# Wider moving blocks for ScalarE's quarter of a layer's product, and a norm's Newton steps on GpSimd

## The chip, the cores and the metric

The kernel runs on one core of a Trainium2 chip. The metric is the device time of one execution in microseconds, from its start to the end of its last output; several executions are timed, and their median counts. A profile of one execution gives the span (first to last instruction), what each engine did when, and what each wait was for. The engines are TensorE (PE in the profile, its weight loads PEld), VectorE (DVE), ScalarE (ACT), GpSimd (POOL) and SyncE (SP), which issues most of the DMAs.

## What is computed

Two graph layers on x of 8 batches, 2048 nodes and 64 features, with one sparse 2048 x 2048 adjacency matrix whose rows are normalized. Layer 0 has weights and a bias of its own for each node, mixed from 16 shared ones by an embedding; layer 1 has one weight for all. Each layer adds its input and is normalized over the features. Cut to what matters:

```python
def _layernorm(x, axis=-1, eps=1e-5):
    m = jnp.mean(x, axis=axis, keepdims=True)
    v = jnp.var(x, axis=axis, keepdims=True)
    return (x - m) / jnp.sqrt(v + eps)

def _L0_gnn_ref(x, A, embedding, weight, bias):      # K = 3, D = 16
    w = jnp.einsum('nd,dkio->nkio', embedding, weight)
    b = jnp.einsum('nd,do->no', embedding, bias)
    # A_stack: identity, A, 2 A A - identity
    x_g = jnp.einsum('knm,bmc->bnkc', A_stack, x)
    return jnp.einsum('bnki,nkio->bno', x_g, w) + b

x = _layernorm(x + _L0_gnn_ref(x, adj, embedding0, weight0, bias0))
x = _layernorm(x + _L1_gnn_ref(x, adj, adj, weight1, bias1))
```

## The kernel before

The program runs in stages: two hops over the adjacency matrix for layer 0, layer 0's product with its weights (lines 394 to 441, called from the loop at 834), and two hops for layer 1. The change is in the product. It goes over 16 tiles of 128 nodes (`t` from 0 to 15).

For a tile, `mix0` multiplies the three inputs (x, first hop, second hop) by the 16 shared weights, and sums over the 16 with each node's embedding as factor. Inputs and weights are split into three parts each (high, low, mixed; `parts` at line 308, `w_parts`), so that an input times a weight is three matmuls. The eight batches lie as four pairs: two batches of a pair are on the lower and the upper 64 partitions, and a matmul uses 64 rows of the array. Matmuls therefore come in pairs `j` = 0, 1, on the two halves of the array, into two neighbouring banks of PSUM.

The work of a tile is cut into eight pieces `(g, dg)`: `g` is a half of the batches (two pairs, `i` = 0, 1) and `dg` a group of DG = 4 of the 16 weights. A piece fills one buffer of two PSUM banks, of which there are four in rotation (`bank`, shared with the transposes `pt` and the projection `pu`). It takes 36 matmuls with 256 moving columns (4 weights of 64 columns): 2 `i` x 3 inputs x 3 parts x 2 `j`. Then it is evicted: with `dg` = 0 by ScalarE (line 429), four operations of 128x256 that scale by the embedding and write to a buffer `aside`; else by VectorE (line 431), four multiply-and-add operations of 128x256 into the accumulator `acc`. In tile 15 ScalarE takes `dg` = 0 and 1. GpSimd folds an `aside` in two steps (line 403: 512, then 256 elements) and adds it to `acc` (line 400).

The order on each engine is as written: in this part of the program `ordered` keeps the recorded order of all instructions but the matmuls, whose order is also that of the source. Each engine takes its instructions strictly in turn, so an instruction that waits holds up all behind it on its engine. The dictionary `at` says which other work is recorded before which piece: the preparation of the next tile's parts (`of_x`, `of_hop`, `of_second`), the steps `n1`, `n2`, `n3` of the previous tile's norm, the start of the next tile's sum (`begin_sum`, GpSimd), the multiplication by the matrix's values (`times_r`, GpSimd), the transposes of the previous tile's normalized rows (`hT`), and in tile 15 the operands of the next stage (`early`, on ScalarE and VectorE, with DMAs from SP). After the pieces the previous tile is projected with layer 1's weights (`project`), and ScalarE copies the result out.

The norm (`layernorm`, line 359) sums a row on VectorE, subtracts the mean on GpSimd, squares on ScalarE, sums the squares on VectorE, takes the root on ScalarE, and then takes 1/root on VectorE and refines it by one Newton step (`rsqrt_parts`, lines 325 to 346; four small VectorE operations of 128x8 besides the reciprocal). GpSimd multiplies by it (line 374).

```python
ds = slice(dg * DG, (dg + 1) * DG)
pm = bank("pm").rearrange("p j (i d c) -> p j i d c", i=2, d=DG)
...
if dg < on_act:
    ordered(nc.scalar.activation(to[:, d], got, AF.Copy, scale=e))
else:
    ordered(nc.vector.scalar_tensor_tensor(part, got, e, part, ALU.mult, ALU.add))
```

Of the kernel before, what the change touches and what calls it, by code (L numbers as in the profile page):

```python
# [9 lines left out]
F32 = mybir.dt.float32  # L10
# [3 lines left out]
AF = mybir.ActivationFunctionType  # L14
ALU = mybir.AluOpType
# [3 lines left out]
P = 128  # L19
B, N, C = 8, 2048, 64  # L20
NT = N // P
D = 16
DG = 4
EPS = 1e-5
# [15 lines left out]
def pattern(  # L40
# [22 lines left out]
    nc = tc.nc  # L63
# [5 lines left out]
    work = pool(ctx, "fwork", 2)  # L69
# [14 lines left out]
    def bank(name):  # L84

        return psum.tile([P, 2, 512], F32, tag="ps", name=name)
# [40 lines left out]
    def ordered(ins):  # L127
        if in_order:
            tc.keep_in_program_order(ins)
# [173 lines left out]
    def transpose(src, tag, pt=None):  # L303

        tt = xcpool.tile([P, B // 2, P], F32, tag="ln_xc", name=tag)
        ordered(nc.scalar.copy(by_half(tt), transposed(src, pt)))
        return tt
# [15 lines left out]
    def wide(c):  # L323
        return c.unsqueeze(2).to_broadcast([P, B, C])

    def rsqrt_parts(ss):


        def col(name):
            m = max(B, ss.shape[1])  # L330
            return (work if m == B else keep).tile(list(ss.shape), F32, tag=f"{name}{m}", name=name)

        va = col("ln_v")
        ordered(nc.vector.scalar_tensor_tensor(va, ss, 1.0 / C, eps.to_broadcast(list(ss.shape)), ALU.mult, ALU.add))
        sd = col("ln_sd")
        ordered(nc.scalar.activation(sd, ss, AF.Sqrt, bias=eps, scale=1.0 / C))
        yield None
        r0 = col("ln_r0")
        ordered(nc.vector.reciprocal(r0, sd))

        q = col("ln_q")
        ordered(nc.vector.scalar_tensor_tensor(q, r0, -0.5, r0, ALU.mult, ALU.mult))
        ordered(nc.vector.tensor_tensor(q, q, va, ALU.mult))
        r = col("ln_r")
        ordered(nc.vector.scalar_tensor_tensor(r, q, 1.5, r0, ALU.add, ALU.mult))
        yield r
# [12 lines left out]
    def layernorm(src):  # L359

        s = work.tile([P, B], F32, tag="ln_s", name="s")
        ordered(nc.vector.tensor_reduce(s, src, AX.X, ALU.add))
        ordered(nc.vector.tensor_tensor(s, s, part, ALU.mult))
        xc = xcpool.tile([P, B, C], F32, tag="ln_xc", name="xc")
        ordered(nc.gpsimd.tensor_tensor(xc, src, wide(s), ALU.subtract))  # L365
        yield xc.rearrange("p b c -> p (b c)")
        sq = squares(xc)
        yield
        ss = work.tile([P, B], F32, tag="ln_ss", name="ss")
        ordered(nc.vector.tensor_reduce(ss, sq, AX.X, ALU.add))  # L370
        root = rsqrt_parts(ss)
        next(root)
        yield
        ordered(nc.gpsimd.tensor_tensor(xc, xc, wide(next(root)), ALU.mult))
        yield

    def store(t, r):
# [13 lines left out]
            ))  # L391
        return acc

    def mix0(t, tt, acc, at, on_act=1):

        aside = [None, None]

        def add_aside(g):
            part = acc[:, 4 * g : 4 * g + 4, :]
            ordered(nc.gpsimd.tensor_tensor(part, part, aside[g][:, 0], ALU.add))  # L400

        def summed(one, other, n):
            ordered(nc.gpsimd.tensor_tensor(one[:, :n], one[:, :n], other, ALU.add))  # L403

        for g in range(2):
            part = acc[:, 4 * g : 4 * g + 4, :]
            for dg in range(D // DG):
                if (g, dg) == (1, 2 if on_act == 1 else 0):
                    add_aside(0)
                for work_here in at.get((g, dg), ()):  # L410
                    work_here()
                ds = slice(dg * DG, (dg + 1) * DG)
                pm = bank("pm").rearrange("p j (i d c) -> p j i d c", i=2, d=DG)
                for i in range(2):
                    for k in range(3):
                        for n in range(3):
                            for j in range(2):
                                q = slice(j * C, (j + 1) * C)
                                nc.tensor.matmul(  # L419
                                    pm[:, j, i], lhsT=tt[k][n][q, 2 * g + i, :], rhs=w_parts[n][k][q, ds, :],  # L420
                                    start=(k == 0 and n == 0), stop=(k == 2 and n == 2),
                                )
                if dg < on_act:
                    to = rawp.tile([P, DG, B // 2, C], F32, tag="raw", name="aside")
                for d in range(DG):
                    dd = dg * DG + d
                    got, e = pm[:, :, :, d, :].rearrange("p j i c -> p (j i) c"), emb_sb[:, t, dd : dd + 1]
                    if dg < on_act:
                        ordered(nc.scalar.activation(to[:, d], got, AF.Copy, scale=e))  # L429
                    else:  # L430
                        ordered(nc.vector.scalar_tensor_tensor(part, got, e, part, ALU.mult, ALU.add))  # L431
                if dg < on_act:
                    if dg == 0:
                        aside[g] = to
                    else:
                        summed(aside[g], to, DG)
                    if dg == on_act - 1:
                        for n in (2, 1):
                            summed(aside[g], aside[g][:, n : 2 * n], n)
        add_aside(1)  # L440
        return layernorm(acc)

    def project(t, hT, pus=None):
# [245 lines left out]
    def times_r(t):  # L689
        to = z2[:, t, :].rearrange("p (j n) -> p j n", n=P)  # L690
        r = rrow[:, t * P : (t + 1) * P].unsqueeze(1).to_broadcast([P, B // 2, P])
        ordered(nc.gpsimd.tensor_tensor(to, to, r, ALU.mult))  # L692
# [9 lines left out]
    def operands(t, quick=False):  # L702

        xt = work2.tile([P, B // 2, P], F32, tag="t0", name="xt")
        load(nc.sync, xt, xT[t])
        tt = [None] * 3

        def begin(k, src):
            where, tag = ((rawp, "raw"), (spool, "s"))[k != 2]
            high = hpool.tile([P, B // 2, P], F32R, tag="hl", name="hl")  # L710
            pair = where.tile([P, 2, B // 2, P], F32R, tag=tag, name="parts")
            tt[k] = [high, pair[:, 0], pair[:, 1]]
            return parts(src, tt[k], by_half if k == 1 else lambda to: to, quick)

        def of_x():
            yield from begin(0, xt)

        def of_hop(pt=None):
            yield from begin(1, transposed(z[1][t], pt))

        def of_second():
            yield from begin(2, by_pair(z[2][t]))

        return tt, of_x(), of_hop, of_second()
# [102 lines left out]
    def go(it):  # L827
        return lambda: next(it)
# [4 lines left out]
    coming = operands(1)  # L833
    for t in range(NT):
        got, last = {}, t == NT - 1
        at = {(g, dg): [] for g in range(2) for dg in range(D // DG)}
        n1, n2, n3 = [lambda: next(norm)] * 3 if t else [nothing] * 3

        if not last:
            following, of_x, of_hop, of_second = coming  # L840
            of_hop = of_hop()
            at[0, 1] += [go(of_x)] * (1 if t else 3)
            at[0, 2] += [go(of_hop), n1, go(of_hop), go(of_hop), n2]
            if t + 2 < NT:
                at[0, 2] += [lambda: times_r(t + 2)]
                at[1, 0] += [lambda: got.update(coming=operands(t + 2))]
            at[0, 3] += [n3, go(of_second), lambda: got.update(acc=begin_sum(t + 1))]
            at[1, 0] += [go(of_second), go(of_second)]
            at[1, 3] += [lambda: got.update(hT=transpose(h, "hT"))] if t else []
        else:  # L850
            at[0, 1] += [n1, lambda: early(0, *y, *s)]
            at[0, 2] += [n2, lambda: early(1, *y, *s)]
            at[0, 3] += [n3, lambda: early(2, *y)]
            at[1, 0] += [lambda: early(3, *y)]
            at[1, 1] += [lambda: early(4, *y)]
            at[1, 2] += [lambda: got.update(hT=transpose(h, "hT"))]
            at[1, 3] += [lambda: project(t - 1, got["hT"])]
        norm_now = mix0(t, tt, acc, at, 2 if last else 1)
        if 0 < t < NT - 1:
            project(t - 1, got["hT"])  # L860
        if "coming" in got:
            coming = got["coming"]
            next(coming[1])
            next(coming[1])
        norm = norm_now
        h = next(norm)
        if not last:
            tt, acc = following, got["acc"]
# [480 lines left out]
```

## Time and profile before

| what | us |
|---|---|
| median of three executions | 769.81 (767.96 to 770.3) |
| the profiled execution | 768.76 |
| its span | 767.0 |
| layer 0's product in it | 226.8 to 533.7 |
| one tile of it, from tile to tile | 19.15 |
| TensorE granted clock | 0.997 of full speed |

Busy times of the engines in one stretch of 19 us inside the product (321 to 340 us): TensorE 19.00, VectorE 16.67, ScalarE 9.43, GpSimd 13.98; DMA engines 6%. The last stretch, 511.0 to 533.6, has TensorE busy 21.0 of 22.6 us.

How to read the lines: a line of a chain gives start, length, engine, tile and source line; a line of a group gives the source line, the engine and operation, output and inputs with their shape (partitions x elements), the count, the busy time and mean duration in ns, and after the second bar the idle time of the engine ahead of them and what ended it. In the timeline a row with "x36" runs from the first instruction's start to the last one's end, and matmuls overlap, so that a row's length is not a sum. Instructions that only wait, or that issue a DMA, are not counted as busy.

### The profile page before, as it was taken

The numbers are of one execution on the slowest core, as the hardware profiler recorded it, in microseconds if no ns is written. First come the engines' busy times: TensorE is split into PE (matmuls) and PEld (weight loads), VectorE is DVE, ScalarE is ACT, GpSimd is POOL, SyncE is SP. The second block draws the span as 40 slices with busy tenths as digits, with TensorE's granted clock in tenths as the row PEclk, the third lists the DMA queues.
The fourth block names the chain that finished last, engine by engine and source line by source line (L and its number), as shares of the span: only waits on it lengthen the run. The fifth ranks groups of instructions, "written<-read, shape, count | busy, mean of one in ns | idle before, by whom it ended". The sixth has DMA issues, their size and how long they took to land.

```text
span 767.0 us, 18011 instructions
## 1 busy us (share of the span) xinstructions
PE 757.0 (99%) x7246; PEld 674.8 (88%) x7246; DVE 582.8 (76%) x1222; ACT 387.7 (51%) x760; POOL 252.5 (33%) x247
## 2 busy tenths in 40 slices
PE   8999999999999999999999999999999999999996
PEld 6888888888889999999999999998888888888886
DVE  6778766677758898888889888876688648668664
ACT  4446533878744555555545555547787763112111
POOL 0000000000026777777777777766100000012341
PEclk9999999999999999999999999999999999999998
DMA  8998996555510000000000000002354444565731
GB/s 308 374 389 294 340 313 209 164 168 164 171 60 27 20 8 19 20 17 16 17 16 10 20 17 3 3 29 70 127 168 146 138 149 137 178 183 164 217 128 45
DMA packets 73546, 96.77 MB, mean 126 GB/s; under 512 B 4848, under 2 KB 48368, under 8 KB 73328
## 3 DMA queue, kind: packets, MB, share of 16 engines
q1 hardware_dynamic: 62048, 76.66, 30.7%
q10 hardware_dynamic: 11408, 18.89, 6.6%
q8 instruction: 59, 0.97, 0.5%
q14 instruction: 31, 0.25, 0.1%
HBM read 76.65 MB, written 18.87 MB: 125 GB/s over the span
## 4 chain that ended last, share of the span: by engine, by line
PE 96%; DVE 2%; DMA 1%; ACT 1%; POOL 0%; issue 0%; SPq 0%; POOLq 0%; DVEq 0%
PE pm L419 35%; PE accT L641 27%; PE acc L254 15%; PE a L254 10%; PE accT L254 6%; PE pu L451 2%; DMA raw<-in_adj 1%; PE pt L300 1%; DVE acc L431 1%; PE accT L791 1%; DVE hl L238 0%; PE accT L451 0%; ACT aside L429 0%; SPq L123 0%; POOL xc L365 0%
## 5 line engine op out<-in xcount | busy, mean ns | idle before, releaser
L419 PE MATMUL pm<-wh,hl 64*128 64x256 f32 x1536 | 235.4, 286 | 0.7 <-DVE acc L431 0.7
L419 PE MATMUL pm<-wm,parts 64*128 64x256 f32 x1536 | 230.9, 280 | 0.0
L419 PE MATMUL pm<-wl,parts 64*128 64x256 f32 x1536 | 230.8, 280 | 0.0
L641 PE MATMUL accT<-s,hl 128*128 128x512 f32 x896 | 205.7, 390 | 0.0
L431 DVE SCALAR_TENSOR_TENSOR acc<-pm,pack_sb,acc 128x256 f32<-128x256 f32 x376 | 181.5, 483 | 27.5 <-PE pm L419 14.1
L641 PEld LDWEIGHTS accT<-s,hl 128*128 128x128 f32 x896 | 167.6, 188 | 35.4 <-issue 0.2
L419 PEld LDWEIGHTS pm<-wh,hl 64*128 64x128 f32 x1536 | 160.3, 188 | 1.2 <-PE pt L300 0.8
L419 PEld LDWEIGHTS pm<-wl,parts 64*128 64x128 f32 x1536 | 160.2, 188 | 0.0
L419 PEld LDWEIGHTS pm<-wm,parts 64*128 64x128 f32 x1536 | 160.0, 187 | 0.0
L629 ACT CAST s<-raw 128x1024 fp32r<-128x1024 bf16 x104 | 109.7, 1055 | 38.0 <-ACT hl L234 24.7
L254 PE MATMUL acc<-hl,s 128*128 128x512 f32 x512 | 117.3, 390 | 0.6 <-DVE s L223 0.6
L254 PEld LDWEIGHTS acc<-hl,s 128*128 128x128 f32 x512 | 95.8, 188 | 21.8 <-issue 1.0
L692 POOL TENSOR_TENSOR z<-z,rrow 128x512 f32<-128x512 f32 x16 | 21.1, 1319 | 213.0 <-DVE z L665 213.0
L429 ACT ACTIVATE aside<-pm,pack_sb 128x256 f32<-128x256 f32 x136 | 53.3, 475 | 54.0 <-PE pm L419 54.0
L234 ACT CAST hl<-z 128x256 fp32r<-128x256 f32 (+1 forms) x96 | 47.4, 511 | 63.4 <-PE acc L254 24.7
L403 POOL TENSOR_TENSOR aside<-aside 128x512 f32<-128x512 f32 (+2 forms) x66 | 70.5, 1068 | 18.4 <-ACT aside L429 15.7
L254 PE MATMUL a<-hl,s 128*128 128x512 f32 (+1 forms) x352 | 73.4, 370 | 0.0
L254 PEld LDWEIGHTS a<-hl,s 128*128 128x128 f32 x352 | 61.9, 188 | 11.3
L238 DVE TENSOR_TENSOR hl<-z,hl 128x512 fp32r<-128x512 f32 (+1 forms) x96 | 54.6, 576 | 14.0 <-ACT hl L234 11.4
L320 POOL TENSOR_TENSOR parts<-parts 128x512 fp32r<-128x512 f32 x45 | 57.7, 1294 | 11.6 <-DVE parts L314 9.8
L287 POOL TENSOR_TENSOR z<-z,got 128x512 f32<-128x512 f32 x3 | 4.8, 1622 | 143.8 <-ACT got L286 143.8
L254 PE MATMUL accT<-hl,s 128*128 128x512 f32 x192 | 44.3, 390 | 0.0
(129 smaller groups left out, 822.9 us busy)
## 6 DMA issues: line engine op xcount, KB each, us to landing
raw<-in_adj SPq DMA_DIRECT2D x59, 512.0 KB, 5.6
raw<-sums_of SPq DMA_DIRECT2D x64, 256.0 KB, 2.7
sums_of<-z ACTq DMA_DIRECT2D x16, 512.0 KB, 6.1
raw<-quarters SPq DMA_DIRECT2D x32, 256.0 KB, 2.7
raw<-in_adj SPq DMA_DIRECT2D x16, 384.0 KB, 3.0
quarters<-seen ACTq DMA_DIRECT2D x16, 256.0 KB, 5.7
xt<-in_xT SPq DMA_DIRECT2D x16, 256.0 KB, 2.6
z<-in_x SPq DMA_DIRECT2D x15, 256.0 KB, 6.9
```

Source lines behind the costliest of these rows:

```text
L234: ordered(nc.scalar.copy(to[0], src))
L238: ordered(nc.vector.tensor_tensor(to[1], src, to[0], ALU.subtract))
L254: nc.tensor.matmul(accs[i], lhsT=s[:, i * P : (i + 1) * P], rhs=hl[h], start=(first and h == 0), stop=(last and h == 1),)
L320: ordered(nc.gpsimd.tensor_tensor(mixed, mixed, low, ALU.add))
L403: ordered(nc.gpsimd.tensor_tensor(one[:, :n], one[:, :n], other, ALU.add))
L419: nc.tensor.matmul(pm[:, j, i], lhsT=tt[k][n][q, 2 * g + i, :], rhs=w_parts[n][k][q, ds, :], start=(k == 0 and n == 0), stop=(k == 2 and n ...
L429: ordered(nc.scalar.activation(to[:, d], got, AF.Copy, scale=e))
L431: ordered(nc.vector.scalar_tensor_tensor(part, got, e, part, ALU.mult, ALU.add))
L451: nc.tensor.matmul(pm[:, j, i * 3 * C : (i + 1) * 3 * C], lhsT=hT[q, 2 * g + i, :], rhs=v[q], start=True, stop=True,)
L629: ordered(nc.scalar.copy(s, got["raw"]))
L641: nc.tensor.matmul(acc[i][:, c], lhsT=hl[h][:, i * P : (i + 1) * P], rhs=S[:, c * 512 : (c + 1) * 512], start=(kk == 0 and h == 0), stop=( ...
L692: ordered(nc.gpsimd.tensor_tensor(to, to, r, ALU.mult))
```

## The change

`mix0` gets a list of pieces instead of two loops. ScalarE's share of a half `g` is now cut by batch, not by weights: piece `(g, 0)` or `(g, 1)` multiplies one pair of batches by eight weights, 512 moving columns, in 18 matmuls, and ScalarE evicts it by eight operations of 128 elements into two `aside` buffers that both pieces of a half share. VectorE's pieces `(g, 2)` to `(g, 5)` are the former `dg` = 0 to 3. In tiles 0 to 14 ScalarE has the two pieces of half 0, at the tile's head and as the fifth piece; all of half 1 goes to VectorE. In tile 15 it has both pieces of both halves. GpSimd folds a half's two buffers in one go (1024, 512, 256 elements and the addition to `acc`), once a tile instead of twice, and ahead of the seventh piece (in tile 15 ahead of the fourth and the eighth).

The norm inside the product no longer calls `rsqrt_parts`: VectorE keeps the reciprocal, and five small operations go to GpSimd. In tile 15 `n3` moves up to the third piece, the transposes to the sixth and the projection to the seventh.

```diff
-        root = rsqrt_parts(ss)
-        next(root)
+        sd, r0, va, q, r = [work.tile([P, B], F32, tag=f"{name}{B}", name=name) for name in ("ln_sd", "ln_r0", "ln_v", "ln_q", "ln_r")]
+        ordered(nc.scalar.activation(sd, ss, AF.Sqrt, bias=eps, scale=1.0 / C))
         yield
-        ordered(nc.gpsimd.tensor_tensor(xc, xc, wide(next(root)), ALU.mult))
+        ordered(nc.vector.reciprocal(r0, sd))
+        ordered(nc.gpsimd.tensor_scalar(va, ss, -0.5 / C, -0.5 * EPS, ALU.mult, ALU.add))
+        ordered(nc.gpsimd.tensor_tensor(q, r0, r0, ALU.mult))
+        ordered(nc.gpsimd.tensor_tensor(q, q, va, ALU.mult))
+        ordered(nc.gpsimd.tensor_scalar(q, q, 1.0, 1.5, ALU.mult, ALU.add))
+        ordered(nc.gpsimd.tensor_tensor(r, q, r0, ALU.mult))
+        ordered(nc.gpsimd.tensor_tensor(xc, xc, wide(r), ALU.mult))
         yield
...
-    def mix0(t, tt, acc, at, on_act=1):
+    def mix0(t, tt, acc, at, pieces):
+        def block(pm, lhsT, ds):
+            for k in range(3):
+                for n in range(3):
+                    for j in range(2):
+                        q = slice(j * C, (j + 1) * C)
+                        nc.tensor.matmul(
+                            pm[:, j], lhsT=tt[k][n][q, lhsT, :], rhs=w_parts[n][k][q, ds, :],
+                            start=(k == 0 and n == 0), stop=(k == 2 and n == 2),
+                        )
...
+        def by_batch(g, i):
+            pm = bank("pm").rearrange("p j (d c) -> p j d c", c=C)
+            block(pm, 2 * g + i, slice(0, 2 * DG))
+            if i == 0:
+                aside[g] = [rawp.tile([P, DG, 2, 2, C], F32, tag="raw", name="aside") for _ in range(2)]
+            for d in range(2 * DG):
+                ordered(nc.scalar.activation(aside[g][d // DG][:, d % DG, :, i, :], pm[:, :, d, :], AF.Copy, scale=e(d)))
+
+        def by_four(g, dg):
+            dg -= 2
+            pm = bank("pm").rearrange("p j (i d c) -> p j i d c", i=2, d=DG)
+            for i in range(2):
+                block(pm[:, :, i], 2 * g + i, slice(dg * DG, (dg + 1) * DG))
+            for d in range(DG):
+                part = acc[:, 4 * g : 4 * g + 4, :]
+                got = pm[:, :, :, d, :].rearrange("p j i c -> p (j i) c")
+                ordered(nc.vector.scalar_tensor_tensor(part, got, e(dg * DG + d), part, ALU.mult, ALU.add))
...
         def add_aside(g):
+            one, other = [a.rearrange("p d j i c -> p d (j i) c") for a in aside[g]]
             part = acc[:, 4 * g : 4 * g + 4, :]
+            for to, more in ((one, other), (one[:, :2], one[:, 2:]), (one[:, 0], one[:, 1]), (part, one[:, 0])):
+                ordered(nc.gpsimd.tensor_tensor(to, to, more, ALU.add))
...
+            at[6] += [0]
+            at[7] += [lambda: got.update(hT=transpose(h, "hT"))] if t else []
+            pieces = [(0, 0), (0, 4), (0, 5), (1, 2), (0, 1), (1, 3), (1, 4), (1, 5)]
         else:
...
+            at[1] += [n1, lambda: early(0, *y, *s)]
+            at[2] += [n2, n3, lambda: early(1, *y, *s)]
+            at[3] += [0, lambda: early(2, *y)]
+            at[4] += [lambda: early(3, *y)]
+            at[5] += [lambda: early(4, *y), lambda: got.update(hT=transpose(h, "hT"))]
+            at[6] += [lambda: project(t - 1, got["hT"])]
+            at[7] += [1]
+            pieces = [(0, 0), (0, 1), (0, 4), (1, 0), (1, 1), (0, 5), (1, 4), (1, 5)]
```

A number in `at` stands for `add_aside` of that half.

More of the change, by code (lines that the diff above doesn't have):

```diff
@@ L392, in begin_sum, with e @@
         return acc
-    def mix0(t, tt, acc, at, on_act=1):
-        aside = [None, None]
+    def mix0(t, tt, acc, at, pieces):
[8 more added lines that the diff above has]
+                        )
+        def e(d):
+            return emb_sb[:, t, d : d + 1]
+        def by_batch(g, i):
[14 more added lines that the diff above has]
+                ordered(nc.vector.scalar_tensor_tensor(part, got, e(dg * DG + d), part, ALU.mult, ALU.add))
+        aside = {}
@@ L398, in add_aside @@
         def add_aside(g):
+            one, other = [a.rearrange("p d j i c -> p d (j i) c") for a in aside[g]]
             part = acc[:, 4 * g : 4 * g + 4, :]
[L400 to L410, printed above, removed]
-                    work_here()
[L412 to L439, printed above, removed]
@@ L440, in mix0 @@
-        add_aside(1)
+            for to, more in ((one, other), (one[:, :2], one[:, 2:]), (one[:, 0], one[:, 1]), (part, one[:, 0])):
+                ordered(nc.gpsimd.tensor_tensor(to, to, more, ALU.add))
+        for n, (g, i) in enumerate(pieces):
+            for work_here in at[n]:
+                if isinstance(work_here, int):
+                    add_aside(work_here)
+                else:
+                    work_here()
+            (by_batch if i < 2 else by_four)(g, i)
         return layernorm(acc)
@@ L835, in pattern @@
         got, last = {}, t == NT - 1
-        at = {(g, dg): [] for g in range(2) for dg in range(D // DG)}
+        at = [[] for _ in range(8)]
         n1, n2, n3 = [lambda: next(norm)] * 3 if t else [nothing] * 3
@@ L841, in pattern @@
             of_hop = of_hop()
-            at[0, 1] += [go(of_x)] * (1 if t else 3)
-            at[0, 2] += [go(of_hop), n1, go(of_hop), go(of_hop), n2]
+            at[1] += [go(of_x)] * (1 if t else 3)
+            at[2] += [go(of_hop), n1, go(of_hop), go(of_hop), n2]
             if t + 2 < NT:
[L845 to L849, printed above, removed]
-        else:
[L851 to L858, printed above, removed]
+                at[2] += [lambda: times_r(t + 2)]
+                at[4] += [lambda: got.update(coming=operands(t + 2))]
+            at[3] += [n3, go(of_second), lambda: got.update(acc=begin_sum(t + 1))]
+            at[4] += [go(of_second), go(of_second)]
+            at[6] += [0]
+            at[7] += [lambda: got.update(hT=transpose(h, "hT"))] if t else []
+            pieces = [(0, 0), (0, 4), (0, 5), (1, 2), (0, 1), (1, 3), (1, 4), (1, 5)]
+        else:
+            at[1] += [n1, lambda: early(0, *y, *s)]
[6 more added lines that the diff above has]
+            pieces = [(0, 0), (0, 1), (0, 4), (1, 0), (1, 1), (0, 5), (1, 4), (1, 5)]
+        norm_now = mix0(t, tt, acc, at, pieces)
         if 0 < t < NT - 1:
```

## The prediction

> **What bounds the kernel now.** I read the page's totals first, then the chain of waits in order of time for the stage that the change touches (226.8 to 533.7 us), then single stretches of the timeline, then the groups kept apart by shape. The totals:
>
> ```profile
> span 767.0 us, 18011 instructions
> PE 757.0 (99%) x7246; PEld 674.8 (88%) x7246; DVE 582.8 (76%) x1222; ACT 387.7 (51%) x760; POOL 252.5 (33%) x247
> ```
>
> TensorE is busy for 99% of the span. That alone doesn't prove a bound, so the chain, here over one tile of layer 0's product and into the next (start, length, what):
>
> ```profile
> 340.48 4.31 PE pm L419 x72
> 345.03 10.85 PE pm L419 x180
> 356.12 2.20 PE pm L419 x36
> 358.32 1.30 PE pu L451 x16
> 359.63 4.31 PE pm L419 x72
> ```
>
> Each link is TensorE's own work, and the same five links repeat every 19.15 us. One tile is 144 pairs of matmuls, 1.30 us of projection and two sets of transposes. So in tiles 0 to 14 only TensorE's own time counts, as long as no buffer comes free late. Its spacing is in the timeline:
>
> ```profile
> 341.25 0.30 PE L419 MATMUL pm<-wm,parts 64*128 64x256 f32 x2
> ...
> 342.45 0.30 PE L419 MATMUL pm<-wh,hl 64*128 64x256 f32 x2
> ...
> 119.63 2.66 PE L254 MATMUL acc<-hl,s 128*128 128x512 f32 x11
> ...
> 579.67 3.11 PE L641 MATMUL accT<-s,hl 128*128 128x512 f32 x13
> ...
> 754.52 6.02 PE L254 MATMUL a<-hl,s 128*128 128x256 f32 x48
> ```
>
> The first two lines are ten pairs apart: 1.20/10 = 120.0 ns a pair of 256 columns. A row of n matmuls lasts (n-1) spacings and one duration (390 ns at 512 columns, 284 at 256, from the groups), so 512 columns take (2.66-0.39)/10 = 227.0 and (3.11-0.39)/12 = 226.7 ns, and 256 columns on the full array (6.02-0.284)/47 = 122.0 ns. Doubling the columns from 122.0 adds 104.7, not 122.0: about 17 ns belong to the matmul, not to its columns.
>
> Two places where TensorE does wait lie in the last tile (waits of this stage: total, times, longest):
>
> ```profile
> PE pt L300 <- POOL xc L374: 0.9, 1, 0.9
> PE pm L419 <- DVE acc L431: 0.7, 1, 0.7
> ```
>
> What prices the other engines' edits is in the groups by shape (busy, mean ns | idle before):
>
> ```profile
> L429 ACT ACTIVATE aside<-pm,pack_sb 128x256 f32<-128x256 f32 x136 | 53.3, 475 | 54.0 <-PE pm L419 54.0
> L403 POOL TENSOR_TENSOR aside<-aside 128x512 f32<-128x512 f32 x32 | 41.6, 1299 | 12.4 <-ACT aside L429 12.2
> L403 POOL TENSOR_TENSOR aside<-aside 128x256 f32<-128x256 f32 x32 | 23.9, 748 | 2.5
> L403 POOL TENSOR_TENSOR aside<-aside 128x1024 f32<-128x1024 f32 x2 | 5.0, 2483 | 3.4 <-ACT aside L429 3.4
> ```
>
> and two lines of the timeline, of which the second shows VectorE held up beside GpSimd:
>
> ```profile
> 370.41 1.04 POOL L374 TENSOR_TENSOR xc<-xc,ln_r 128x512 f32<-128x512 f32 x1 [0.51 <-DVE ln_r L345]
> ...
> 520.50 2.25 DVE L238 TENSOR_TENSOR hl<-z,hl 128x256 fp32r<-128x256 f32 x1 [1.67 <-ACT hl L234]
> ```
>
> **What the Trainium skill says.** "TensorE: Matmul & The Clock Gate", section "Back-to-back issue gap", gives N/2.4 + 2.5 ns for an isolated matmul: 109.2 at 256 columns, 215.8 at 512. The trace agrees that there is a fixed part and has it larger: 120.0 and 226.7. "VectorE: DVE Perf Modes", in its section on the TRN2 errata, prices a ScalarE operation out of PSUM at 172 cycles plus one per element at 1.2 GHz: 357 ns at 256, 250 at 128; the trace has 365 at 256 ((1.57-0.475)/3 in a row of four). "SBUF — State Buffer", section "SBUF: two separate sides", says that GpSimd and a VectorE operation with two SBUF inputs exclude each other for a whole instruction. The trace agrees: the VectorE line above took 2.25 us where its kind takes 0.42, beside a GpSimd addition of 1024 elements.
>
> **The change, part by part.**
>
> *Moving blocks.* In tiles 0 to 14 two of eight pieces become 9 pairs of 512 columns in place of 18 of 256; in tile 15 four do. The trace has no pair of 512 columns on half arrays, so I bound it. Not cheaper per column: 240.0 ns, no gain. At the skill's 215.8: 24.2 gained a pair. I take 226.7, what a 512-column matmul costs here on the full array, because at 256 columns the half-array pair (120.0) and the full-array matmul (122.0) cost nearly the same. Gain: 240.0-226.7 = 13.3 ns a pair, 18 x 13.3 = 239 ns a tile, 15 x 0.239 = 3.6 us. The tile goes from 19.15 to 18.91 us.
>
> *ScalarE's eviction.* 8 operations of 128 elements a piece instead of 4 of 256: 8 x 0.25 + 0.1 = 2.1 us against 1.57, twice a tile, some 1 us more on an engine that is busy 9.6 of 19 us. Piece 0's bank is wanted again by piece 3, 4.6 us after piece 0 ends: 2.5 us are spare. Piece 4's, by piece 7, has about as much.
>
> *GpSimd's sums.* Before: 2 x (1.299 + 0.748 + 0.769) = 5.63 us a tile. After: 2.483 + 1.299 + 0.748 + 0.769 = 5.30 us, all behind piece 4's eviction (done 13.1 us into the tile) and behind the second hop's parts (15.4): they end at 20.7, that is 1.8 us into the next tile. The next norm's sum reads the accumulator, but stands on VectorE behind a subtraction that waits for ScalarE until 1.7 and ends at 2.4 (361.99 before, in a tile begun at 359.63). So 0.5 us are spare; beyond that the delay is still only VectorE's, which waits 1.1 us for TensorE there.
>
> *Newton steps.* VectorE loses four operations (in the timeline 0.27+0.43+0.17+0.17 = 1.0 us). GpSimd gains five on 128x8. No such row exists there: the slope of the additions is (1299-748)/256 = 2.15 ns an element, which leaves some 0.2 us fixed; GpSimd's fills of 128x1 took 0.1; the 128x256 addition, 0.75, is an upper bound. I take 0.25, so 1.2 us. Because the old sums are gone from the time before it, the Newton chain starts at 9.7 and the multiplication of xc at 10.9, against 370.41-359.63 = 10.8 now. TensorE reads xc at 15.2: hidden, 3 us spare. VectorE, a microsecond earlier, meets the bank that it owes the projection earlier than now.
>
> *Last tile.* Fixed: 36 pairs x 13.3 = 0.48 us gained. Order: xc's transposes are now ahead of the sixth piece (10.3 us in), and ScalarE's list is four evictions of 2.1 us among casts. Counting it on: piece 1 evicted 8.2, root 8.5, GpSimd's steps and multiplication to 11.0: TensorE waits 0.7 (0.9 now). Then the copy of the transposes is behind piece (1,1)'s eviction, 14.2, and ends at 15.1, where the projection wants it at 13.4: a new wait of 1.7 us in place of 1.1 (0.7 and 0.4 of issue). Then VectorE's sums of the sixth piece wait for GpSimd's first accumulator addition (16.7) and end at 18.7, just when the last piece wants that bank. The tile then ends at 20.8 to 21.0; now it takes 533.7-512.7 = 21.0 (from the end of the projection begun at 511.4 to L641's first). I count 0.1 us gained, with 1 us either way.
>
> Sum: 3.6 + 0.1 = 3.7 us. The profiled execution took 768.76 us (span 767.0, 1.76 around it), so 765.1; it lies 1.05 us below the median shown, 769.81. Set against that median: 766.1.
>
> **Rivals.**
>
> *Half arrays pay per column.* If the 13 ns of a pair come from streaming, a 512-column pair takes 240 ns and nothing is gained; VectorE's microsecond was off the path. 769.8. For it: 120.0 and 240 would be exact proportion; against: 122.0 and 226.7 on the full array are not.
>
> *The fixed part goes altogether* (215.8): 18 x 24.2 x 15 = 6.5 and 0.9 in the last tile, less its waits: about 762.8. Against it: no 512-column row in the trace is below 226.
>
> *GpSimd becomes the bound (slower).* Its loop from one norm's sum to the next is 14.1 us of operations in the new order (1.05 + 3 x 1.29 + 1.32 + 1.05 + 2 x 0.755 + 5.30), 1.0 for the two VectorE steps between, some 0.7 of hand-offs, 15.8 in all, and five small operations. It paces the tile once one costs over (18.91-15.8)/5 = 0.62 us, and loses from (19.15-15.8)/5 = 0.67. At the upper bound of 0.75 a tile takes 19.55: 15 x 0.40 = 6 us more, 776. For it: GpSimd is busy 14.0 of 19 us already, and every small step waits for the one before. Against: the fill took 0.1.
>
> *The last tile eats it.* If the waits there total 3 us more, the result is within 0.3%: 769.
>
> **How the numbers follow.** The forecast gets 0.64: 0.56 of it beyond 0.3% (2.3 us, about what a measurement of this kernel can tell from no change), 0.08 within. The vanished fixed part gets 0.08, all faster; pay per column and the last tile together 0.16, of which 0.14 within and 0.02 slower; GpSimd's bound 0.12, slower. That makes faster 0.64, within 0.3% 0.22, slower 0.14. The range runs from the vanished fixed part, 762.8, to no gain and a little more, 770.6; it leaves out most of GpSimd's case and a sliver on the fast side.
>
> **What would show it.** Right: the chain through tiles 1 to 14 still all TensorE, a period near 18.91 us, ten 512-column pairs in 2.27 us, evictions of 128 elements spaced 0.25, small GpSimd steps near 0.25, no wait of TensorE before tile 15. Wrong: a 512-column pair at 240; TensorE waiting for xc, for a bank that ScalarE or VectorE holds, or for GpSimd in every tile; tile 15 longer than 22 us.

## The result and the profile after

The changed kernel takes 766.64 us (median of 7 runs, 765.88 to 767.44) where the kernel before, run beside it, takes 768.87. The ratio is 0.997, with a 95% interval from 0.9958 to 0.9981: faster by 0.3%, 2.2 us, and by 1.5 to 3.2 us within the interval. The profiled execution took 767.01 us, its span 765.1. The totals of the page after:

```profile
span 765.1 us, 16925 instructions
PE 754.4 (99%) x6634; PEld 660.1 (86%) x6634; DVE 561.1 (73%) x1158; ACT 406.4 (53%) x896; POOL 269.8 (35%) x297
```

There are 612 matmuls fewer (16 tiles, 36 each, and 36 more in the last one), VectorE is 21.7 us less busy, ScalarE 18.7 and GpSimd 17.3 more. TensorE alone went with the span, 2.6 us less busy at a span 1.9 shorter. The chain of waits after, over one tile and into the next (start, length, what):

```profile
339.77 4.22 PE pm L409 x54
344.00 0.24 PE pt L300 x8
344.24 10.75 PE pm L409 x162
354.99 0.24 PE pt L300 x8
355.23 2.20 PE pm L409 x36
357.43 1.30 PE pu L460 x16
358.73 4.22 PE pm L409 x54
```

It is still TensorE's own work without a gap. A tile is 358.73 - 339.77 = 18.96 us, 0.19 less than the 19.15 before. The two links that hold a piece of 512 columns became shorter, 4.31 to 4.22 and 10.85 to 10.75, and the others are as they were. By the matmuls' starts in the two traces, the product as a whole (first matmul of `pm` to the first of `accT` behind it) went from 306.84 to 304.06 us, so 2.8 less: 15 x 0.19 = 2.9 from tiles 0 to 14, and the last tile 0.16 longer, 21.14 for 20.98. The remaining 0.9 us between this and the span's 1.9 lie in the stages ahead of and behind the product, which the change doesn't touch (the product began at 227.3 for 226.8, and what follows it took 233.8 for 233.3). In the traces of the experiments below, where those earlier stages are the same too, the product begins anywhere from 226.2 to 227.3.

The head of a tile in the timeline of the kernel after:

```profile
358.79 0.40 PE L409 MATMUL pm<-wl,parts 64*128 64x512 f32 x2
359.02 0.40 PE L409 MATMUL pm<-wm,parts 64*128 64x512 f32 x2
...
360.41 0.40 PE L409 MATMUL pm<-wm,parts 64*128 64x512 f32 x2
360.64 0.29 PE L409 MATMUL pm<-wh,hl 64*128 64x256 f32 x2
```

From the first of these lines to the last are eight pairs of 512 columns: (360.64 - 358.79)/8 = 231 ns each. The forecast took 226.7. The tile's other wide piece, which stands between narrow pairs, is nearer to it:

```profile
348.44 0.40 PE L409 MATMUL pm<-wh,hl 64*128 64x512 f32 x2
...
349.60 0.40 PE L409 MATMUL pm<-wm,parts 64*128 64x512 f32 x2
...
350.51 0.28 PE L409 MATMUL pm<-wh,hl 64*128 64x256 f32 x2
```

Its first five pairs take (349.60 - 348.44)/5 = 232 ns each, the other four (350.51 - 349.60)/4 = 227.

What the other engines do, first ScalarE at the head of the second tile and then GpSimd over the first:

```profile
360.86 2.18 ACT L423 ACTIVATE aside<-pm,pack_sb 128x128 f32<-128x128 f32 x8 [0.46 <-PE pm L409]
```

```profile
349.48 0.20 POOL L375 TENSOR_SCALAR ln_v<-ss 128x8 f32<-128x8 f32 x1
349.64 0.20 POOL L376 TENSOR_TENSOR ln_q<-ln_r 128x8 f32<-128x8 f32 x1
...
350.77 1.05 POOL L380 TENSOR_TENSOR xc<-xc,ln_r 128x512 f32<-128x512 f32 x1
...
354.89 4.57 POOL L441 TENSOR_TENSOR aside<-aside 128x1024 f32<-128x1024 f32 x3
359.54 0.75 POOL L441 TENSOR_TENSOR acc<-acc,aside 128x256 f32<-128x256 f32 x1
362.07 1.04 POOL L365 TENSOR_TENSOR xc<-acc,s 128x512 f32<-128x512 f32 x1 [1.78 <-DVE s L363]
```

The five Newton steps last 350.77 - 349.48 = 1.29 us, and the multiplication starts 11.0 us into its tile (339.77) and ends 3.2 us ahead of the transposes that read it, at 354.99. The fold ends at 360.29, which is 1.6 us into the next tile (358.73). TensorE waits for none of it. Its only waits in the product, in the view of waits between 226 and 536 us (engine, who releases it, total, times, longest), are in tile 15:

```profile
PE pu L460 <- ACT hT L306: 1.5, 1, 1.5
...
PE pt L300 <- POOL xc L380: 0.6, 1, 0.6
```

Each occurs once. The wait on VectorE's bank, 0.7 before, is gone, the one on the normalised columns is 0.6 for 0.9, and the one on the copy of the transposes is new.

### The profile page after: what moved, and what is told of

Same layout as the page of the kernel before. It is cut to its first block, busy times and chain, and to the rows that moved or that the text cites. A ratio compares the mean times of both kernels' runs of the same rounds, so it can differ in the third digit from the quotient of the medians.

```text
span 765.1 us, 16925 instructions
## 1 busy us (share of the span) xinstructions
PE 754.4 (99%) x6634; PEld 660.1 (86%) x6634; DVE 561.1 (73%) x1158; ACT 406.4 (53%) x896; POOL 269.8 (35%) x297
## 4 chain that ended last, share of the span: by engine, by line
PE 96%; ACT 2%; DMA 1%; DVE 0%; SPq 0%; issue 0%; DVEq 0%
PE pm L409 35%; PE accT L650 27%; PE acc L254 15%; PE a L254 10%; PE accT L254 6%; PE pu L460 3%; ACT aside L423 1%; DMA raw<-in_adj 1%; PE pt L300 1%; PE accT L800 1%; ACT s L638 0%; PE accT L460 0%; ACT hl L234 0%; SPq L123 0%; PE accT L153 0%; PE accT L300 0%
## 5 line engine op out<-in xcount | busy, mean ns | idle before, releaser
L409 PE MATMUL pm<-wh,hl 64*128 64x256 f32 (+1 forms) x1332 | 208.1, 303 | 0.0
L409 PE MATMUL pm<-wm,parts 64*128 64x256 f32 (+1 forms) x1332 | 203.5, 296 | 0.0
L409 PE MATMUL pm<-wl,parts 64*128 64x256 f32 (+1 forms) x1332 | 203.4, 296 | 0.0
L409 PEld LDWEIGHTS pm<-wh,hl 64*128 64x128 f32 x1332 | 130.9, 187 | 4.0 <-issue 0.4
L409 PEld LDWEIGHTS pm<-wl,parts 64*128 64x128 f32 x1332 | 130.7, 187 | 3.7
L409 PEld LDWEIGHTS pm<-wm,parts 64*128 64x128 f32 x1332 | 130.5, 187 | 3.8
L423 ACT ACTIVATE aside<-pm,pack_sb 128x128 f32<-128x128 f32 x272 | 74.4, 395 | 48.1 <-PE pm L409 48.1
L441 POOL TENSOR_TENSOR aside<-aside 128x1024 f32<-128x1024 f32 (+2 forms) x51 | 75.2, 1475 | 2.7
L238 DVE TENSOR_TENSOR hl<-z,hl 128x512 fp32r<-128x512 f32 (+1 forms) x96 | 56.0, 591 | 13.4 <-ACT hl L234 10.8
```

Source lines behind the costliest of these rows:

```text
L238: ordered(nc.vector.tensor_tensor(to[1], src, to[0], ALU.subtract))
L409: nc.tensor.matmul(pm[:, j], lhsT=tt[k][n][q, lhsT, :], rhs=w_parts[n][k][q, ds, :], start=(k == 0 and n == 0), stop=(k == 2 and n == 2),)
L423: ordered(nc.scalar.activation(aside[g][d // DG][:, d % DG, :, i, :], pm[:, :, d, :], AF.Copy, scale=e(d)))
L441: ordered(nc.gpsimd.tensor_tensor(to, to, more, ALU.add))
```

## The experiments

Each kernel is the changed one with the edit shown, and was timed against the kernel before, which took 769.01 us beside the first four and 768.87 beside the other four. "Period" is the time from one tile's projection to the next one's in the profiled execution.

### The blocks alone taken back

The pieces stay ScalarE's, in the same order and evicted by the same eight operations, but are multiplied in two blocks of 256 columns.

```diff
-            block(pm, 2 * g + i, slice(0, 2 * DG))
+            for h in range(2):
+                block(pm[:, :, h * DG : (h + 1) * DG], 2 * g + i, slice(h * DG, (h + 1) * DG))
```

> The changed kernel with its order, its evictions and its GpSimd steps, but ScalarE's pieces multiplied in two blocks of 256 columns each. Theory (the whole gain is the width of the moving blocks on TensorE): the tile returns from 18.96 to 19.15 us, the product is 3.0 us longer, the time is that of the kernel before, 768.9 within 1 us, or up to 1 us more for the last tile, whose new waits stay while its 0.4 us of width go. Rival (VectorE freed of four small operations and of a fold twice a tile is what helps): the tile stays near 18.96 and the time near 766.6.

Measured: 769.14 us, ratio 0.9999 (0.9991 to 1.0007). In its chain of waits the projections are back at the old distance:

```profile
377.47 1.30 PE pu L461 x16
...
396.62 1.30 PE pu L461 x16
```

396.62 - 377.47 = 19.15 us. Without the width nothing is left of the gain, so all else in the change together (Newton steps, order of the pieces, folding) is worth nothing that can be measured, in either direction: the interval is some 0.6 us to each side.

### The Newton steps back on VectorE

```diff
-        sd, r0, va, q, r = [work.tile([P, B], F32, tag=f"{name}{B}", name=name) for name in ("ln_sd", "ln_r0", "ln_v", "ln_q", "ln_r")]
-        ordered(nc.scalar.activation(sd, ss, AF.Sqrt, bias=eps, scale=1.0 / C))
+        root = rsqrt_parts(ss)
+        next(root)
...
+        r = next(root)
```

> The changed kernel with the norm's Newton steps back on VectorE. Theory: they are off the path in tiles 1 to 14 wherever they run; tile 18.96, time 766.6 within 0.7. In tile 15 VectorE does them behind the root, a little sooner than GpSimd (three operations of 0.17 against four of 0.28): up to 0.4 us less wait for xc there, given back at ScalarE's copy. Rival (GpSimd's steps free VectorE for TensorE's banks): TensorE waits for a bank of VectorE in each tile, 19.1 us or more a tile, 768.9.

Measured: 767.14 us, ratio 0.9967 (0.9955 to 0.9978), period 18.96, as in the changed kernel. So VectorE's microsecond was off the path and so is GpSimd's. Only tile 15 is longer, 21.78 for 21.14 us in the one profile of each: VectorE is late there with a bank, a wait of 0.7 us that the changed kernel doesn't have. The shorter wait for the normalised columns that was expected there didn't come (0.7 us for 0.6).

### Every piece in blocks of 512

VectorE's pieces are multiplied in 512 columns too, and evicted as before, so that the values in a bank are those of other batches and weights than its eviction takes them for; the sums are not the product's.

```diff
-            for i in range(2):
-                block(pm[:, :, i], 2 * g + i, slice(dg * DG, (dg + 1) * DG))
+            wide_pm = pm.rearrange("p j i d c -> p j (i d c)")
+            block(wide_pm, 2 * g + dg % 2, slice(dg // 2 * 2 * DG, (dg // 2 + 1) * 2 * DG))
```

> The changed kernel with VectorE's six pieces in 512 columns too (eight weights of one pair of batches), evicted by the same four operations of 128x256 as before; it computes other sums than the product asks for, with the same number of operations of each kind on VectorE, ScalarE and GpSimd. All 72 pairs of a tile have 512 columns. Theory (a pair of 512 columns costs 227 ns when it follows its like, the first few after narrower ones up to 9 more): 72 x 13 = 0.94 us a tile against the kernel before, so 18.2 us a tile, 0.75 less than in the changed kernel, 16 tiles: 766.6 - 11.5 = 755. Rival (a 512-column pair of half arrays costs 231 wherever it stands): 72 x 9 = 0.65 a tile, 18.5, 759. Rival (width is not the cause): 766.6.

Measured: 756.67 us, ratio 0.9833 (0.9819 to 0.9846). The chain of waits has a period of 388.85 - 370.48 = 18.37 us, between the two expectations:

```profile
370.48 1.30 PE pu L460 x16
...
388.85 1.30 PE pu L460 x16
```

This shows what a pair gains, in two doses. From before to after 18 pairs of a tile are widened: (19.15 - 18.96)/18 = 10.6 ns each. From after to this kernel another 54: (18.96 - 18.37)/54 = 10.9 ns each. A pair of 512 columns therefore takes 240.0 - 10.8 = 229 ns, not 226.7. The timeline shows where the difference is. Here a row of such pairs behind a set of transposes, from its second pair on:

```profile
431.38 0.40 PE L409 MATMUL pm<-wl,parts 64*128 64x512 f32 x2
...
433.24 0.39 PE L409 MATMUL pm<-wh,hl 64*128 64x512 f32 x2
...
434.14 0.39 PE L409 MATMUL pm<-wl,parts 64*128 64x512 f32 x2
...
436.41 0.39 PE L409 MATMUL pm<-wm,parts 64*128 64x512 f32 x2
```

The first eight spacings average (433.24 - 431.38)/8 = 232 ns, the ten from 434.14 on (436.41 - 434.14)/10 = 227 ns. A wide row behind transposes thus reaches the full-array figure only after some eight pairs. In the changed kernel a row is nine pairs long in tiles 0 to 14: the one at the tile's head, behind the projection, is nearly all beginning, and the other is so for five pairs of nine. This is not a matter of half arrays. By the matmuls' starts in the trace of the kernel before, the full-array row right behind the product (512 columns, from 533.98 on) begins with spacings of 236, 228, 233 and 230 ns and keeps to 227 after that.

### The last tile in another order

In tile 15 the norm's second step moves from ahead of the third piece to ahead of the second, (0,5) ahead of (1,1), the first fold two pieces later, and the second fold behind all pieces.

```diff
+        for half in sum(at[len(pieces):], []):
+            add_aside(half)
...
-            at[1] += [n1, lambda: early(0, *y, *s)]
-            at[2] += [n2, n3, lambda: early(1, *y, *s)]
-            at[3] += [0, lambda: early(2, *y)]
+            at[1] += [n1, lambda: early(0, *y, *s), n2]
+            at[2] += [n3, lambda: early(1, *y, *s)]
+            at[3] += [lambda: early(2, *y)]
...
-            at[5] += [lambda: early(4, *y), lambda: got.update(hT=transpose(h, "hT"))]
+            at[5] += [0, lambda: early(4, *y), lambda: got.update(hT=transpose(h, "hT"))]
...
-            at[7] += [1]
-            pieces = [(0, 0), (0, 1), (0, 4), (1, 0), (1, 1), (0, 5), (1, 4), (1, 5)]
+            at += [[1]]
+            pieces = [(0, 0), (0, 1), (0, 4), (1, 0), (0, 5), (1, 1), (1, 4), (1, 5)]
```

> The changed kernel with tile 15 in another order: the root ahead of the second piece's eviction, VectorE's piece (0, 5) ahead of ScalarE's (1, 1), the transposes between them so that their copy is ahead of the last eviction, GpSimd's addition of half 0 after (0, 5), that of half 1 at the end. Theory (tile 15 of the changed kernel loses 2.2 us of TensorE to waits that its order makes: 0.6 for xc and 1.5 for the copy of the transposes): tile 15 goes from 21.0 to 18.6 to 19.2 us, time 766.6 - 2.1 = 764.5. Rival (the waits turn up elsewhere, at the bank that VectorE's sums hold or at the next stage's operands): 766.6 or more.

Measured: 765.36 us, ratio 0.9946 (0.9932 to 0.9959), below both kernels by its median. The last tile takes 20.16 us for 21.14, less of a gain than expected. Its view of waits has two smaller ones in place of the changed kernel's:

```profile
PE pm L409 <- DVE acc L433: 0.7, 1, 0.7
PEld pu L462 <- ACT hT L306: 0.5, 1, 0.5
```

### Five more steps on GpSimd, and twelve

Steps of 128x8, each on the one before, are put between the fourth Newton step and the last, in the norms of tiles 0 to 13, that is in every norm that is finished in the product but the last one. They rewrite the tile that they read, with its own values.

```diff
-    def layernorm(src):
+    def layernorm(src, more=0):
...
+        for _ in range(more):
+            ordered(nc.gpsimd.tensor_scalar(q, q, 1.0, 0.0, ALU.mult, ALU.add))
...
-        return layernorm(acc)
+        return layernorm(acc, 5 if t < NT - 2 else 0)
```

> The changed kernel with five more small steps (128x8, each on the one before) on GpSimd in the norm of every tile but the last; they rewrite a scratch tile. Theory (GpSimd has room: from its rows in the changed kernel its loop per tile is the period 18.96 less what it idles, 16.8 us, and five steps at 0.285 us add 1.4, so 18.2, still below the period): period 18.96, time 766.6, no change against the changed kernel. Rival (GpSimd's delay of the normalised columns already reaches TensorE): 1.4 us a tile, some 20 us in all, 785.

Measured: 766.51 us, ratio 0.9967 (0.9954 to 0.9979), period 18.96. Five more cost nothing in these tiles. In tile 15, which finishes a norm without them, the wait for the normalised columns is 1.1 us for 0.6 in the profile, and the tile 0.5 us longer; the medians don't show it.

The next kernel has `12` in place of `5`.

> The same with twelve more small steps in each of 14 norms. Theory: GpSimd's loop is 16.84 + 12 x 0.285 = 20.26 us, longer than the period by 1.3, so the tile takes about 20.3 and the kernel about 785 (14 x 1.3 = 18 us more); the turning point lies at about seven steps. Rival (GpSimd's loop never sets the period, the columns are wanted late enough): 766.6. Second rival (the cover is gone earlier than I count, all twelve steps are paid): 14 x 3.4 = 48 us more, 814.

Measured: 791.32 us, ratio 1.0288 (1.0273 to 1.0303), period 20.66. It is slower by 24.7 us than the changed kernel, between the theory's 18 and the second rival's 48. TensorE now waits in every tile. In the view of waits between 226 and 536 us (the product ends at 555.9):

```profile
PE pt L300 <- POOL xc L382: 19.5, 14, 1.5
```

The chain of waits of this kernel, which in the changed one is all TensorE's, is led by GpSimd ("POOL aside L443 23.7%"). Its timeline over one period of GpSimd:

```profile
400.14 3.66 POOL L380 TENSOR_SCALAR ln_q<-ln_q 128x8 f32<-128x8 f32 x12
403.88 0.20 POOL L381 TENSOR_TENSOR ln_r<-ln_q,ln_r 128x8 f32<-128x8 f32 x1
404.16 1.04 POOL L382 TENSOR_TENSOR xc<-xc,ln_r 128x512 f32<-128x512 f32 x1
...
414.60 1.04 POOL L365 TENSOR_TENSOR xc<-acc,s 128x512 f32<-128x512 f32 x1 [1.06 <-DVE s L363]
...
424.82 1.04 POOL L382 TENSOR_TENSOR xc<-xc,ln_r 128x512 f32<-128x512 f32 x1
```

From the first of the twelve steps to the Newton step behind them are 403.88 - 400.14 = 3.74 us. Taken off the period of 20.66 they leave 16.9: that is the changed kernel's loop through GpSimd. My expectation for this run had 16.84 for it and 12 x 0.285 = 3.4 us for the steps, 0.4 us a tile too little in all, 14 x 0.4 = 6 us, which is what it missed. Nearly all of that is one step. The others start 0.28 us apart, but in each of the 14 norms one (here the fourth) lasts 0.52 to 0.60 us. It runs beside a VectorE subtraction with two SBUF operands; here the step as the chain has it, then VectorE's timeline:

```profile
400.97 0.60 POOL ln_q L380
```

```profile
400.83 0.68 DVE L314 TENSOR_TENSOR parts<-z,hl 128x512 fp32r<-128x512 f32 x1
```

The wait of 1.06 ahead of line 365 stays though GpSimd is late: it is VectorE's sum and the small step behind it, which belong to the loop. With 16.9, TensorE's 18.96 leave 2.0 us, six or seven steps more (at 0.31 and at 0.28 each), which agrees with five free and twelve paid in part.

### Two of VectorE's pieces in blocks of 512

On the kernel with the reordered last tile, the pieces (0,4) and (0,5) of tiles 0 to 14 are also cut by batch, and VectorE evicts each by eight operations of 128 elements instead of four of 256.

```diff
+        def by_batch_late(g, i):
+            pm = bank("pm").rearrange("p j (d c) -> p j d c", c=C)
+            block(pm, 2 * g + i, slice(2 * DG, 4 * DG))
+            part = acc.rearrange("p (g j i) c -> p g j i c", g=2, j=2)[:, g, :, i, :]
+            for d in range(2 * DG):
+                ordered(nc.vector.scalar_tensor_tensor(part, pm[:, :, d, :], e(2 * DG + d), part, ALU.mult, ALU.add))
...
-            (by_batch if i < 2 else by_four)(g, i)
+            late = t < NT - 1 and g == 0 and i > 3
+            (by_batch if i < 2 else by_batch_late if late else by_four)(g, i - 4 * late)
```

> On the reordered last tile (765.4): VectorE's two last pieces, (0,4) and (0,5), are also multiplied in blocks of 512 in tiles 0 to 14 and evicted by eight VectorE instructions of 128 elements each; sums are the reference's. Theory: 18 pairs more at 10.8 ns are 0.19 us a tile, 14 to 15 tiles, so 2.8 us less, 762.5, if VectorE (15.3 of 18.96 us busy) can take the some 1.7 us a tile that twelve more instructions cost. Rival: VectorE releases the banks late, TensorE waits for them at a tile's head, 765.4 or slower.

Measured: 771.98 us, ratio 1.0038 (1.0024 to 1.0051), period 19.22: the rival, and slower than the kernel before. The timeline of VectorE shows the price, and that of GpSimd where it goes:

```profile
402.10 0.69 DVE L362 TENSOR_REDUCE s<-acc 128x8 f32<-128x512 f32 x1 [1.45 <-POOL acc L448]
...
402.90 3.05 DVE L430 SCALAR_TENSOR_TENSOR acc<-pm,pack_sb,acc 128x128 f32<-128x128 f32 x8
...
407.07 3.04 DVE L430 SCALAR_TENSOR_TENSOR acc<-pm,pack_sb,acc 128x128 f32<-128x128 f32 x8
410.03 0.19 DVE L374 RECIPROCAL ln_r<-ln_sd 128x8 f32<-128x8 f32 x1
...
421.33 0.69 DVE L362 TENSOR_REDUCE s<-acc 128x8 f32<-128x512 f32 x1 [1.45 <-POOL acc L448]
```

```profile
410.30 0.20 POOL L376 TENSOR_TENSOR ln_q<-ln_r 128x8 f32<-128x8 f32 x1 [0.76 <-DVE ln_r L374]
...
411.44 1.04 POOL L380 TENSOR_TENSOR xc<-xc,ln_r 128x512 f32<-128x512 f32 x1
```

A piece's eviction takes VectorE 3.05 us for 2.0, so the eight operations more (the expectation counts twelve) cost 2.1 us a tile. Both evictions stand between the sum and the reciprocal in VectorE's order: the reciprocal comes 410.03 - 402.10 = 7.9 us after the sum, and GpSimd waits 0.76 us for it. The chain of waits runs round this loop, 421.33 - 402.10 = 19.23 us from one sum to the next, and the period is 19.22. (The 16.9 of the run with twelve steps and these 2.1 make 19.0, but that is no proof: there the loop ran through GpSimd's own work ahead of the Newton steps, not over these evictions.) VectorE is busy only 16.60 us of the period. What sets the period is not one engine but the round from the sum over VectorE's evictions, the reciprocal, GpSimd's steps, its parts and its fold back to the accumulator, for which the next sum waits 1.45 us.

### The casts of the last tile in another place

On the same kernel with the reordered last tile, without the two wide pieces. The expectation calls the new place earlier; in VectorE's order the edit puts the cast that stood ahead of the eviction of (0,4) behind it, in front of later evictions:

```diff
-            at[2] += [n3, lambda: early(1, *y, *s)]
-            at[3] += [lambda: early(2, *y)]
+            at[2] += [n3]
+            at[3] += [lambda: early(1, *y), lambda: early(2, *y)]
+            at[7] += [lambda: early(1, *s)]
```

> On the reordered last tile (765.4): in the last tile the casts of the next product's operands are put earlier in VectorE's order, so that VectorE evicts (0,4) and copies without them in front. Theory: the two waits left in the last tile (0.67 us on VectorE's bank of (0,4), 0.5 on the copy of the transposes) shrink by 0.7 to 1.2 us together, 764.4. Rival: the casts in their new place delay another eviction, and the wait only moves: 765.4.

Measured: 765.03 us, ratio 0.995 (0.9938 to 0.9963), no different from the reordered kernel's 0.9946. The rival holds: the wait moved. In this kernel's waits:

```profile
PE pm L409 <- DVE acc L433: 1.1, 1, 1.1
```

It is now for the bank of (0,5), for these lines of the two engines stand beside each other:

```profile
518.58 4.40 DVE L238 TENSOR_TENSOR hl<-z,hl 128x256 fp32r<-128x256 f32 x3 [0.25 <-ACT hl L234]
522.90 2.03 DVE L433 SCALAR_TENSOR_TENSOR acc<-pm,pack_sb,acc 128x256 f32<-128x256 f32 x4
```

```profile
518.63 4.93 POOL L441 TENSOR_TENSOR aside<-aside 128x1024 f32<-128x1024 f32 x3
```

Three subtractions with two SBUF operands, 0.41 to 0.43 us each where they stand alone, last 4.40 beside the fold. VectorE takes its work in the order written: the eviction of (0,5), whose last pair of matmuls started at 519.88, stands behind them and starts at 522.90.

## Why the prediction was right

**The bound, shown.** It said that in tiles 0 to 14 only TensorE's own time counts. The chain after, and the run with the blocks taken back (769.14 us, no gain), show it.

**Moving blocks, right in kind, over-sized.** The prediction put a pair of 512 columns at 226.7 ns, the full-array matmul's, for a gain of 13.3 ns a pair and 3.6 us in all. Two doses of the width measured 10.6 and 10.9 ns. 15 tiles x 18 pairs x 10.8 = 2.9 us, 0.7 less than counted. The term that was mis-sized is the price of a pair: the middle of a long row was taken for rows of nine, whose first five to eight pairs take some 232 ns. The full-array rows of the kernel before begin slowly too, so its trace could have told. The rival that half arrays pay per column (240 ns, no gain) and the one that the fixed part goes altogether (215.8) both fall. One reading was off without consequence: the 122.0 ns of a full-array matmul of 256 columns include the first spacing of that row, 0.22 us. By the starts in the trace the spacing is 120.0 from the sixth on, as on half arrays, so that 512 columns add 106.7 ns and about 13 ns, not 17, belong to the matmul.

**ScalarE's eviction, right.** 2.18 us for an estimate of 2.1, and no wait on its banks in tiles 0 to 14.

**GpSimd, right.** The fold ends 1.6 us into the next tile (1.8 forecast), the multiplication starts at 11.0 (10.9), a small step takes 0.20 us and 0.26 from start to start (0.25). The loop was put at 15.8 us and five small steps, so 17.1 with the measured 0.26; the run with twelve more gives 16.9. The slower rival, GpSimd as the bound, was thus a real mechanism with its turning point in the right place (six or seven steps more), and fell only because a step costs 0.26 us and not the 0.62 from which it would have decided.

**The Newton steps leaving VectorE, right at nothing.** Putting them back changes no period. In the last tile it may help that they are gone: with them back the tile is 0.64 us longer in one profile, while the medians, 767.14 and 766.64, don't tell the two apart.

**The last tile, right in its waits.** The normalised columns: 0.7 forecast, 0.6 measured. The copy of the transposes: 1.7 and 1.5. VectorE's sums behind GpSimd's first addition to the accumulator: a wait, too. The tile was to be 20.8 to 21.0 us, 0.1 less than before, and is 21.14, 0.16 more: the other sign, but within the microsecond allowed, and far from the 3 us of the rival in which the last tile eats the gain.

**The sum.** 3.7 us was forecast. With 2.9 for the blocks and -0.16 for the last tile the traces give 2.8, and the medians 2.2 with an interval up to 3.2. That the forecast time, 766.1, lies only 0.5 us below the measured one is in part luck: the gain was over-counted by 1.5 us, and set against a median of three runs (769.81) that lies 0.9 above the one measured beside the changed kernel.

**What is shown and what isn't.** Shown: that the width is the gain, its price per pair, that neither VectorE's nor GpSimd's share of the Newton steps matters in tiles 0 to 14, and where GpSimd's and VectorE's room ends. Not settled: why the first pairs of a wide row are slower (half arrays are not the reason), and whether the fixed part that a merged pair saves belongs to its matmuls or to their weight loads, of which a merged pair also has half as many. Weight loads alone don't set the 120 ns: at the transposes eight loads of 64x128 ran within 0.38 us (343.73 in the changed kernel).

## What to carry to other kernels

Where TensorE bounds a stage with short matmuls, wider moving blocks gain a fixed time per matmul merged away: measure it in rows as long as the kernel's own and behind the same kind of work, and then ask which engine pays for the other cut of the result, because eight evictions in place of four were free on ScalarE and cost more than the width brought on VectorE. Before adding work to an engine beside the bound, count the loop that its work closes from tile to tile, over all engines on it and with the evictions that stand between: the busy share says little of the room. GpSimd, 35% busy on the page, was idle 3.8 us of a tile of the product, and could use some 2.0 of them (18.96 - 16.9); VectorE, idle 3.7, couldn't take 2.1 more where they were put.

## What the runs showed of the hardware

A pair of half-array matmuls of 512 columns starts some 232 ns after the one before in the first eight or so of a row behind transposes or a projection, in the first five behind pairs of 256, and 227 ns later on. Full-array rows of 512 columns begin slowly too, 228 to 236 ns before 227. Of 256 columns a pair takes 120.0 ns in the middle of a row in both kernels.

A GpSimd operation on 128x8 lasts 0.20 us and starts 0.28 us after the one whose result it reads.

A VectorE multiply-and-add out of PSUM takes 2.0 us for four of 256 elements and 3.05 for eight of 128, so 0.5 us and 0.38: half the elements save a quarter of the time.

"SBUF — State Buffer", section "SBUF: two separate sides", in the Trainium skill has GpSimd and a VectorE operation with two SBUF inputs exclude each other. The last experiment agrees: three such operations took 4.40 us beside GpSimd's fold, for 0.41 to 0.43 each alone, and by the starts and lengths in its trace the second and the third end 0.29 us after one of the fold's additions ends. So does the run with twelve steps, where the GpSimd operation is the one that waits, 0.60 us for 0.20.
